# Group 3's x in the first stream of loads, pair 3's selection beside pair 2's, group 2's sums on VectorE, and a new order of VectorE's first steps

## The chip, the core and the metric

The kernel runs on one core of a Trainium2 chip. The core has TensorE (PE in the profile), VectorE (DVE), ScalarE (ACT), GpSimd (POOL) and SyncE (SP), which here issues nearly all transfers; 16 DMA engines carry these out. The metric is device time in microseconds (us). The kernel before has a median of 272.37 us over 3 runs (272.14 to 272.92). A single execution of it was profiled, and all durations below come from that one.

## What is computed

```python
def cond(x, weights, condition):
    W = weights[condition]                       # one 64x64 matrix per batch
    return jnp.einsum('bct,bcd->bdt', x, W)      # x: (64, 64, 1024) float32

def ffn(h, qweight, scale, zero_point, bias):
    w = (unpacked - zero_point) * scale          # unpacked: 6-bit integers, (1024, 1024)
    return jnp.einsum('bsk,nk->bsn', h, w) + bias

out = x + ffn(cond(x, cond_weights, itok), qweight, scale, zero_point, bias)
```

Two products follow each other: a small one with a matrix chosen for each batch, and a large one with quantized weights that are the same for all. The weights stay 6-bit integers in the large product. Their zero point comes in as a correction: the sum of h over its features, times zero point and scale.

## The kernel before, in words

**Tiling.** Two batches of 64 channels make a pair that fills 128 partitions. There are 32 pairs, and two pairs are a group (group g holds pairs 2g and 2g+1). For each pair TensorE does two stages. Stage 1 (line 442; for pairs 0 and 1 line 388) multiplies x by the chosen matrix into PSUM, in a buffer called ph of which there is one from pair 2 on. Stage 2 (line 466) multiplies the result h by the unpacked weights into po, in two banks of 512 columns, with 8 tiles of the contraction. For accuracy h is split into a float16 high part hh (ScalarE, line 454) and a low part hl (VectorE, line 458), and both are multiplied. From pair 2 on x is split in the same way: ScalarE takes magnitudes (line 251), a tiny matmul spreads them (line 255), VectorE makes powers of two (lines 131 to 135), ScalarE writes hf (line 275), VectorE lf (line 285). Four transfers then stack hf and lf into xa (lines 297 to 303), the operand of stage 1.

**The matrices.** The table tab of all 16 matrices is scaled on VectorE (lines 183 and 189). For each pair from 2 on, `select_pair` (line 220) issues two transfers from tab into wst (line 227), one for each batch.

**The sums.** hf's sum over time comes with line 275 as xs. `split_sums` (line 305) splits it into high and low parts xh: ScalarE casts (line 309), then either POOL subtracts (line 311, group 1 alone) or ScalarE does four small activations (line 315). `feature_sums` (line 318, matmuls at line 323) multiplies xh by the chosen matrices, and `unscale_sums` (line 334) scales the result on VectorE.

**The output.** For the first four pairs `early_out` (lines 422 and 426) reads po on VectorE. Later pairs use lines 507 and 512. POOL adds bias and zero points into x (lines 495 and 502), and SP stores.

**The order of work** is written out by hand: each engine executes what the program lists for it, in that order. Lines 533 to 658 are the start, up to the second stage of pair 2 and the first of pair 3. From there `window(p)` (line 663) is called for each pair p from 3 on: TensorE does stage 1 of pair p+1 and then stage 2 of pair p. In windows with even p (p = 2g) the x of group g+3 is loaded and the matrices of group g+2 are selected.

**SP's queue.** SP issues in program order. A transfer takes the semaphore that the eighth transfer before it had, and its issue waits until that one has landed. The first stream (lines 85 to 97) holds, in this order, the condition numbers, the matrices, pair 0's x in two halves, pair 1's x, the weight words in three pieces, the x of pairs 2 and 3, scale and zero point spread over the partitions, and group 2's x. Group 3's x is loaded at line 592, between pair 2's selection and pair 3's pieces of xa; pair 3's selection (line 609) comes behind those pieces.

**The first steps.** 43 dummy matmuls (line 525) keep TensorE busy before x is there. Pairs 0 and 1 use x unsplit with matrices copied by POOL (line 349). VectorE takes the largest weight (line 354), the largest x of the second half (line 368), their product (line 371), and powers from it (line 132); it unpacks the weight words (lines 146 and 148) and writes the low parts of pairs 0 and 1 (line 403).

Of the kernel before, what the change touches and what calls it, by code (L numbers as in the profile page):

```python
# [9 lines left out]
F16 = mybir.dt.float16  # L10
# [4 lines left out]
ALU = mybir.AluOpType  # L15
# [14 lines left out]
def adaln_ffn(ctx: ExitStack, tc: tile.TileContext, x, cond, cw, qw, ws, wz, bias, out):  # L30
# [6 lines left out]
    NG = NP // 2  # L37
    KT = T // P
    LO, HI = slice(0, C), slice(C, P)
    WARM = 43  # L40

    xf = x.rearrange("(i j) c t -> (j c) i t", j=2)
    of = out.rearrange("(i j) c t -> (j c) i t", j=2)
# [23 lines left out]
    def load_x(g):  # L67
        xts[g] = xp.tile([P, 2, T], F32, name="xt")
        nc.sync.dma_start(xts[g], xf[:, 2 * g : 2 * g + 2, :])
# [25 lines left out]
    nc.sync.dma_start(scb, ws.rearrange("n o -> (n o)").partition_broadcast(P))  # L95
    nc.sync.dma_start(zsb, wz.rearrange("n o -> (n o)").partition_broadcast(P))
    load_x(2)


    dummy = const.tile([P, P], BF, name="dummy")  # L100
# [40 lines left out]
    def unpack(kt, n=1):  # L141

        w = kt if kt < 2 else kt - 2 if kt < 6 else kt - 4
        to, of_ = q16[:, kt : kt + n, :], qr[:, w : w + n, :]
        if kt in (2, 3, 6, 7):
            nc.vector.tensor_scalar(to, of_, 6 if kt < 4 else 8, 63, ALU.logical_shift_right, ALU.bitwise_and)  # L146
        else:
            nc.vector.tensor_scalar(to, of_, 63, None, ALU.bitwise_and)  # L148
# [30 lines left out]
    def weights_powers():  # L179
        powers(tmp["pw"], wup, wdn)  # L180
# [39 lines left out]
    def select_pair(p):  # L220
        g, i = divmod(p, 2)
        if i == 0:
            wsts[g] = sp.tile([P, 2, 2, 2, D], F16, name="wst")
        if p not in conditions:
            conditions_of(p)
        for j, k in enumerate(conditions[p]):
            nc.sync.dma_start(wsts[g][:, i, :, j, :], tab[:, ds(k, 1), :, :].rearrange("p o a d -> p (o a) d"))  # L227
# [9 lines left out]
    def magnitudes(g, i):  # L237
        if g not in st:
            st[g] = {
                "l1": sp.tile([P, 2], BF, name="l1"),  # L240
                "u": sp.tile([P, 2], F32, name="u"),
                "hs": sp.tile([P, 2], F32, name="hs"),
                "xs": sp.tile([P, 2], F32, name="xs"),
                "up": sp.tile([P, 2], F32, name="up"),
                "down": sp.tile([P, 2], F32, name="down"),
                "hf": ap.tile([P, 2, T], F16, name="hf"),
                "lf": ap.tile([P, 2, T], F16, name="lf"),
                "xa": ap.tile([P, 2, 2, T], F16, name="xa"),
            }
        junk = ap.tile([P, T], BF, name="junk", bufs=1)  # L250
        nc.scalar.activation(junk, xts[g][:, i, :], AF.Abs, accum_out=st[g]["l1"][:, i : i + 1])  # L251
# [31 lines left out]
    def split_2(g, i, ts_=ALL):  # L283

        nc.vector.scalar_tensor_tensor(  # L285
            st[g]["lf"][:, i, ts_],
            xts[g][:, i, ts_],
            st[g]["down"][:, i : i + 1],
            st[g]["hf"][:, i, ts_],
            ALU.mult,  # L290
            ALU.subtract,
        )
# [9 lines left out]
        nc.sync.dma_start(xa[HI, sl, 0, ts_], lf[LO, sl, ts_])  # L302
        nc.sync.dma_start(xa[LO, sl, 1, ts_], lf[HI, sl, ts_])

    def split_sums(g):
        xs = st[g]["xs"]
        xh = sp.tile([P, 2, 2], F16, name="xh")
        for j, (h, o) in enumerate(((LO, HI), (HI, LO))):
            nc.scalar.copy(xh[h, :, j], xs[h, :])  # L309
            if g == 1:  # L310
                nc.gpsimd.tensor_tensor(xh[o, :, j], xs[h, :], xh[h, :, j], ALU.subtract)  # L311
                continue
            for i in range(2):
                s = slice(i, i + 1)
                nc.scalar.activation(xh[o, s, j], xh[h, s, j], AF.Identity, bias=xs[h, s], scale=-1.0)  # L315
        st[g]["xh"] = xh

    def feature_sums(g):
        xh = st[g]["xh"]
# [31 lines left out]
    def early_weights(p):  # L351

        wl = const.tile([P, 1], F32, name=f"wl{p}")
        nc.vector.tensor_reduce(wl, wbd[:, p, :], AX.X, ALU.max, apply_absolute_value=True)
        nc.vector.tensor_scalar(wm[:, p, :], half, wl[:, 0:1], None, ALU.mult)
# [5 lines left out]
    def early_magnitudes(p, n, ts_, eng):  # L361

        xm[p, n] = const.tile([P, 1], F32, name=f"xm{p}{n}")
        if eng is nc.scalar:
            junk = ap.tile([P, T], BF, name="junk", bufs=1)
            nc.scalar.activation(junk[:, ts_], xts[0][:, p, ts_], AF.Abs, accum_out=xm[p, n])
        else:
            nc.vector.tensor_reduce(xm[p, n], xts[0][:, p, ts_], AX.X, ALU.max, apply_absolute_value=True)

    def early_rows(p, n):  # L370
        nc.vector.tensor_scalar(pb[:, p, n, :], wm[:, p, :], xm[p, n][:, 0:1], LEAST, ALU.mult, ALU.max)
# [14 lines left out]
    def early_stage1(p, ph, kts=range(KT)):  # L386
        for kt in kts:
            nc.tensor.matmul(
                ph[:, kt % ph.shape[1], :, :], lhsT=xts[0][:, p, ts(kt, P)], rhs=wbd[:, p, :], start=True, stop=True
            )  # L390

    def early_high(p, ph, kts):
        if p not in hs_pair:
            hs_pair[p] = [hp.tile([P, KT, P], F16, name="hh"), hp.tile([P, KT, P], F16, name="hl")]
        for j, h in enumerate((LO, HI)):
            nc.scalar.activation(
                hs_pair[p][0][:, kts, h], ph[:, :, j, :], AF.Copy, scale=updown[:, p, 1, j : j + 1]
            )

    def early_low(p, ph, kts):  # L400
        hh, hl = hs_pair[p]
        for j, h in enumerate((LO, HI)):
            nc.vector.scalar_tensor_tensor(  # L403
                hl[:, kts, h], ph[:, :, j, :], updown[:, p, 1, j : j + 1], hh[:, kts, h], ALU.mult, ALU.subtract
            )
# [50 lines left out]
    def stage1_low(p, ph, kts=slice(0, KT)):  # L456
        hh, hl = hs_pair[p]
        nc.vector.tensor_tensor(hl[:, kts, :], ph[:, kts, :], hh[:, kts, :], ALU.subtract)  # L458
# [78 lines left out]
    early_weights(0)  # L537
    early_magnitudes(0, 0, HALF[0], nc.scalar)
    early_stage1(0, ph0a, range(0, 4))
    early_rows(0, 0)  # L540
    early_magnitudes(0, 1, HALF[1], nc.vector)
    early_rows(0, 1)
    early_stage1(0, ph0b, range(4, 6))
    early_bounds(0, 2)
# [1 line left out]
    early_scales(0)  # L546
    early_high(0, ph0a, LOWER)
    early_high(0, ph0b, UPPER)
    unpack(0)
    early_stage1(1, ph1)  # L550
    weights_turn()
    early_weights(1)
    unpack(1)
    early_low(0, ph0a, LOWER)
    stage2_tiles(0, range(0, 2), [0])
    weights_diagonal()
    early_low(0, ph0b, UPPER)
    early_magnitudes(1, 0, ALL, nc.scalar)
    weights_bounds()
    stage2_tiles(0, range(0, 2), [1])  # L560
    early_sums(0)
    unpack(2, 2)
    weights_powers()
    early_rows(1, 0)
    stage2_tiles(0, range(2, 3))
# [22 lines left out]
    unpacking.close()  # L588
    late = ctx.enter_context(tc.tile_pool(name="late", bufs=1))
    select_pair(2)  # L590
    magnitudes(1, 1)
    load_x(3)


    stage2_tiles(1, range(0, 4), [0])
# [10 lines left out]
    stack_low(1, SECOND)  # L606
    early_out(0)
    magnitudes(2, 0)
    select_pair(3)
    nc.sync.dma_start(bib, bias.partition_broadcast(P))  # L610
    select_pair(4)
    select_pair(5)
# [3 lines left out]
    ph = stage1(2)  # L616
    stage1_high(2, ph)
    magnitudes(2, 1)
    split_sums(1)
    stage2_tiles(1, range(7, KT))  # L620
    early_feature_sums(1)
    stage1_low(2, ph)
# [19 lines left out]
    stage1_high(3, ph)  # L642
    early_out(1)
    magnitudes(3, 0)
    magnitudes(3, 1)
    split_sums(2)
    early_zero_points(2)
    stage2_bank(2, 1)
    stage1_low(3, ph)
    split_2(2, 1)  # L650
    stack_high(2, SECOND)
    stack_low(2, SECOND)
# [10 lines left out]
    def window(p):  # L663

        g, i = divmod(p, 2)
        if p + 1 < NP:
            ph = stage1(p + 1)
        if i == 1 and g + 2 < NG:
            bounds(g + 2)
        if i == 1 and g + 1 < NG:  # L670
            feature_sums(g + 1)
        if p - 1 < 4:
            early_out(p - 1)
        else:
            scale_out(p - 1)
        if i == 1 and g + 2 < NG:
            scales_in_full(g + 2)
        if i == 1 and g + 1 < NG:
            unscale_sums(g + 1)
        if p + 1 < NP:  # L680
            stage1_high(p + 1, ph)
        if p - 1 >= 4:
            accumulate(p - 1)
            store(p - 1)
        if p + 1 < NP:
            stage1_low(p + 1, ph)
        if i == 0:
            if g + 3 < NG:
                load_x(g + 3)
            if g + 1 < NG:  # L690
                split_sums(g + 1)
            if g + 2 < NG:
                magnitudes(g + 2, 0)
                magnitudes(g + 2, 1)
            if g + 1 < NG:
                add_bias(p + 2)
                add_bias(p + 3)
            if g + 2 < NG:
                select(g + 2)
        else:  # L700
            if g + 2 < NG:
                for n in range(2):
                    split_1(g + 2, n)
                    split_2(g + 2, n)
                stack_high(g + 2)
                stack_low(g + 2)
            if g + 1 < NG:
                zero_points(p + 1)
                zero_points(p + 2)
        if p in LATE:  # L710

            what, n = LATE[p]
            what(n)
            if what is early_add:
                store(n)
        if p < NP - 1:
            stage2(p)
# [72 lines left out]
```

## Time and profile before

| | |
|---|---|
| median of 3 runs | 272.37 us |
| the profiled execution | 271.98 us |
| its span | 270.2 us |
| TensorE busy | 261.1 us, 97% of the span |
| VectorE, ScalarE, POOL busy | 201.4, 159.3, 166.2 us |
| TensorE busy, by stretches | 5.87 of 6 in 24 to 30, 1.04 of 3 in 30 to 33, 5.26 of 6 in 33 to 39 |
| group 3's x: issue, time to landing | 22.02 us, 7.3 us |
| group 2's x: issue, time to landing | 7.99 us, 11.4 us |
| pair 3's selection: issues, time to landing | 25.29 and 26.04 us, 6.7 and 6.0 us |

The busy row adds up whole stretches with different limits, so a share of 97% doesn't say where the idle 3% lie; the stretches do. A transfer's time to landing is counted from the start of its issue and holds its wait in the queue behind earlier transfers.

### The profile page before, as it was taken

Reading aid. Unit: us, or ns where it says so; the run is one execution under the profiler, and the core shown is the slowest. Engines: PE = TensorE matmul, PEld = TensorE weight load, DVE = VectorE, ACT = ScalarE, POOL = GpSimd, SP = SyncE. Lnnn points to the kernel's source line nnn. Section 1 sums busy time; section 2 is a strip of 40 time slices with the busy share of each in tenths; the row PEclk is TensorE's granted clock in tenths of the full one; section 3 lists DMA queues with packets and bytes.
Section 4 is the critical chain, followed back from the end, with each engine's and each line's share of the span. In section 5 each row is a group of like instructions: output and inputs, shape, how many; then the busy total and the mean of one; then the engine's idle time right before and its main releaser. Section 6 shows DMA issues by size and latency. Waiting matters only on the chain.

```text
span 270.2 us, 5723 instructions
## 1 busy us (share of the span) xinstructions
PE 261.1 (97%) x2161; PEld 140.0 (52%) x2161; DVE 201.4 (75%) x269; ACT 159.3 (59%) x285; POOL 166.2 (61%) x85
## 2 busy tenths in 40 slices
PE   7999789999999999999999999999999999999994
PEld 7645445455555545555554555555455555545553
DVE  3797699498695959869595986959598695955543
ACT  3787698676565667656566765656676565634100
POOL 4000163949689595968959596895919387495200
PEclk9999999999999999999999999999999999999999
DMA  6977876866766797586955797667976764551203
GB/s 220 405 270 183 216 160 190 237 186 186 212 168 231 235 266 238 129 310 187 311 170 158 247 251 238 188 222 243 272 239 173 209 179 146 166 158 78 80 17 139
DMA packets 35708, 54.78 MB, mean 203 GB/s; under 512 B 18400, under 2 KB 18656, under 8 KB 35680
## 3 DMA queue, kind: packets, MB, share of 16 engines
q1 hardware_dynamic: 35648, 54.41, 66.9%
q8 instruction: 17, 0.28, 0.4%
q14 instruction: 11, 0.09, 0.1%
q10 hardware_dynamic: 32, 0.00, 0.0%
HBM read 19.93 MB, written 16.78 MB: 136 GB/s over the span
## 4 chain that ended last, share of the span: by engine, by line
PE 85%; DMA 6%; DVE 4%; SPq 3%; issue 1%
PE po L466 72%; PE ph L442 10%; DMA xt<-in_x_dram 3%; PE pe L466 3%; DMA qr<-in_L_ffn_qweight_dram 2%; DMA xa<-lf 1%; SPq L227 1%; DVE hl L403 1%; PE pu L323 1%; DVE q L148 1%; DVE lf L285 0%; SPq L65 0%; DVE q L146 0%; DVE wsc L183 0%; DVE tab L189 0%
## 5 line engine op out<-in xcount | busy, mean ns | idle before, releaser
L466 PE MATMUL po<-q,hh 128*128 128x512 f16 x496 | 118.5, 379 | 0.4 <-DVE q L146 0.2
L466 PE MATMUL po<-q,hl 128*128 128x512 f16 x496 | 118.5, 379 | 0.0
L502 POOL TENSOR_TENSOR xt<-xt,zt 128x1024 f32<-128x1024 f32 x28 | 78.8, 2833 | 53.1 <-ACT zt L500 53.1
L466 PEld LDWEIGHTS <-hl 128*128 128x128 f16 x520 | 50.6, 98 | 59.1
L495 POOL TENSOR_TENSOR xt<-xt,bib 128x1024 f32<-128x1024 f32 x32 | 75.4, 2379 | 7.5 <-DMA wst<-tab 5.5
L454 ACT CAST hh<-ph 128x1024 f16<-128x1024 f32 x30 | 30.3, 1011 | 82.6 <-PE ph L442 44.8
L466 PEld LDWEIGHTS <-hh 128*128 128x128 f16 x520 | 48.2, 98 | 52.8 <-issue 0.8
L507 DVE SCALAR_TENSOR_TENSOR po<-po,u,scb 128x1024 f32<-128x1024 f32 x27 | 34.7, 1287 | 50.7 <-PE po L466 50.7
L285 DVE SCALAR_TENSOR_TENSOR lf<-xt,down,hf 128x1024 f16<-128x1024 f32 x30 | 62.4, 2117 | 1.8 <-ACT hf L275 1.8
L458 DVE TENSOR_TENSOR hl<-ph,hh 128x1024 f16<-128x1024 f32 x30 | 36.4, 1214 | 0.0
L442 PEld LDWEIGHTS <-xa 128*128 128x128 f16 x960 | 32.1, 98 | 7.9 <-DMA xa<-lf 0.8
L275 ACT ACTIVATE hf<-xt,down 128x1024 f16<-128x1024 f32 x30 | 34.2, 1144 | 2.5 <-DVE down L132 2.5
L512 DVE TENSOR_TENSOR xt<-po,xt 128x1024 f32<-128x1024 f32 x27 | 33.1, 1225 | 2.2 <-DVE po L507 0.5
L442 PE MATMUL ph<-wst,xa 128*128 128x64 f16 x960 | 33.1, 193 | 0.7 <-DMA xa<-lf 0.7
L251 ACT ACTIVATE junk<-xt 128x1024 bf16<-128x1024 f32 x30 | 31.7, 1056 | 1.0 <-DMA xt<-in_x_dram 0.3
L500 ACT ACTIVATE zt<-zsc,hs 128x1024 f32<-128x1024 f32 x28 | 30.5, 1138 | 0.0
L315 ACT ACTIVATE xh<-xh,xs 64x1 f16<-64x1 f16 x56 | 13.4, 287 | 0.9
L311 POOL TENSOR_TENSOR xh<-xs,xh 64x2 f16<-64x2 f32 x2 | 0.4, 194 | 21.0 <-ACT xh L309 20.9
L431 POOL TENSOR_TENSOR xt<-xt,res 128x1024 f32<-128x1024 f32 x4 | 9.4, 2359 | 0.0
L466 PE MATMUL pe<-q,hh 128*128 128x256 f16 (+1 forms) x24 | 6.6, 308 | 0.0
L466 PE MATMUL pe<-q,hl 128*128 128x256 f16 (+1 forms) x24 | 6.5, 308 | 0.0
L334 DVE SCALAR_TENSOR_TENSOR hs<-pu,u 64x2 f32<-64x2 f32 x30 | 4.6, 153 | 1.7 <-PE pu L323 1.6
(83 smaller groups left out, 104.8 us busy)
## 6 DMA issues: line engine op xcount, KB each, us to landing
out_dram<-xt SPq DMA_DIRECT2D x31, 512.0 KB, 3.0
xt<-in_x_dram SPq DMA_DIRECT2D x14, 1024.0 KB, 7.3
xa<-hf SPq DMA_DIRECT2D x26, 256.0 KB, 3.8
xa<-lf SPq DMA_DIRECT2D x26, 256.0 KB, 3.8
wst<-tab SPq DMA_DIRECT2D x60, 32.0 KB, 3.0
xt<-in_x_dram SPq DMA_DIRECT2D x3, 512.0 KB, 7.7
xa<-hf SPq DMA_DIRECT2D x8, 128.0 KB, 2.4
xa<-lf SPq DMA_DIRECT2D x8, 128.0 KB, 3.0
```

The costliest lines, as they stand in the source:

```text
L251: nc.scalar.activation(junk, xts[g][:, i, :], AF.Abs, accum_out=st[g]["l1"][:, i : i + 1])
L275: nc.scalar.activation(st[g]["hf"][:, i, ts_], xts[g][:, i, ts_], AF.Copy, scale=st[g]["down"][:, i : i + 1], accum_out=st[g]["xs"][:, i : ...
L285: nc.vector.scalar_tensor_tensor(st[g]["lf"][:, i, ts_], xts[g][:, i, ts_], st[g]["down"][:, i : i + 1], st[g]["hf"][:, i, ts_], ALU.mult, ...
L442: nc.tensor.matmul(ph[:, kt, j, :], lhsT=st[g]["xa"][:, i, j, ts(kt, P)], rhs=wsts[g][:, i, a, j, :], start=(a == 0), stop=(a == 1),)
L454: nc.scalar.copy(hs_pair[p][0][:, kts, :], ph[:, kts, :])
L458: nc.vector.tensor_tensor(hl[:, kts, :], ph[:, kts, :], hh[:, kts, :], ALU.subtract)
L466: nc.tensor.matmul(po[:, a], lhsT=hs_pair[p][k][:, kt, :], rhs=qT[:, kt, c], start=(kt == 0 and k == 0), stop=(kt == KT - 1 and k == 1),)
L495: nc.gpsimd.tensor_tensor(xt, xt, bib, ALU.add)
L500: nc.scalar.activation(zt, zsc, AF.Copy, scale=st[g]["hs"][:, i : i + 1])
L502: nc.gpsimd.tensor_tensor(xt, xt, zt, ALU.subtract)
L507: nc.vector.scalar_tensor_tensor(po, po, st[g]["u"][:, i : i + 1], scb[:, cols], ALU.mult, ALU.mult)
L512: nc.vector.tensor_tensor(xts[g][:, i, cols], po, xts[g][:, i, cols], ALU.add)
```

## The change

Seven edits. The dummy matmuls grow from 43 to 49. Group 3's x is loaded right behind group 2's, in the first stream. Pair 3's selection is issued right behind pair 2's, ahead of pair 3's pieces of xa. VectorE's first steps are put in another order: the reduction of x's second half ahead of the first row product, pair 1's weights ahead of the first unpacking, and the unpacking of tiles 2 and 3 ahead of the upper half of pair 0's low part. `split_sums` is taken apart into `sums_high` (the two casts) and `sums_low` (the subtraction, on an engine that is given). Group 2's high part stands between the two magnitudes of group 3, and its low part is subtracted on VectorE behind pair 3's hl. Group 1 stays on POOL and groups from 3 on stay on ScalarE, where the two casts now come ahead of the four activations.

```diff
-    WARM = 43
+    WARM = 49
...
     load_x(2)
+    load_x(3)
...
-    def split_sums(g):
-        xs = st[g]["xs"]
-        xh = sp.tile([P, 2, 2], F16, name="xh")
+    def sums_high(g):
+        st[g]["xh"] = sp.tile([P, 2, 2], F16, name="xh")
+        for j, h in enumerate((LO, HI)):
+            nc.scalar.copy(st[g]["xh"][h, :, j], st[g]["xs"][h, :])
+
+    def sums_low(g, eng):
+        xs, xh = st[g]["xs"], st[g]["xh"]
         for j, (h, o) in enumerate(((LO, HI), (HI, LO))):
-            nc.scalar.copy(xh[h, :, j], xs[h, :])
-            if g == 1:
-                nc.gpsimd.tensor_tensor(xh[o, :, j], xs[h, :], xh[h, :, j], ALU.subtract)
+            if eng is not nc.scalar:
+                eng.tensor_tensor(xh[o, :, j], xs[h, :], xh[h, :, j], ALU.subtract)
                 continue
             for i in range(2):
                 s = slice(i, i + 1)
                 nc.scalar.activation(xh[o, s, j], xh[h, s, j], AF.Identity, bias=xs[h, s], scale=-1.0)
-        st[g]["xh"] = xh
...
     early_stage1(0, ph0a, range(0, 4))
+    early_magnitudes(0, 1, HALF[1], nc.vector)
     early_rows(0, 0)
-    early_magnitudes(0, 1, HALF[1], nc.vector)
     early_rows(0, 1)
...
     early_high(0, ph0b, UPPER)
+    early_weights(1)
     unpack(0)
     early_stage1(1, ph1)
     weights_turn()
-    early_weights(1)
     unpack(1)
...
     weights_diagonal()
-    early_low(0, ph0b, UPPER)
     early_magnitudes(1, 0, ALL, nc.scalar)
...
     unpack(2, 2)
+    early_low(0, ph0b, UPPER)
     weights_powers()
...
     select_pair(2)
+    select_pair(3)
     magnitudes(1, 1)
-    load_x(3)
...
     magnitudes(2, 0)
-    select_pair(3)
...
     magnitudes(2, 1)
-    split_sums(1)
+    sums_high(1)
+    sums_low(1, nc.gpsimd)
...
     magnitudes(3, 0)
+    sums_high(2)
     magnitudes(3, 1)
-    split_sums(2)
     early_zero_points(2)
     stage2_bank(2, 1)
     stage1_low(3, ph)
+    sums_low(2, nc.vector)
     split_2(2, 1)
...
             if g + 1 < NG:
-                split_sums(g + 1)
+                sums_high(g + 1)
+                sums_low(g + 1, nc.scalar)
```

## The prediction

> **What bounds the kernel now.** I read three views, in this order. First the chain of waits: from 37.99 us on it is TensorE and nothing else, pair after pair (0.93 us of line 442, 6.9 us of line 466), to the last stores. So whatever this change does in the first 38 us moves the end one for one, unless a later transfer becomes late. Before 37.99 the chain runs through two transfers:
>
> ```profile
> 20.89 0.31 SPq L227
> ...
> 22.02 7.27 DMA xt<-in_x_dram
> 29.28 0.02 issue
> 29.30 0.63 SPq L227
> ...
> 34.19 3.67 DMA xa<-lf
> 37.85 0.14 issue
> 37.99 1.03 PE ph L442 x30
> ```
>
> The reader is to see that group 3's x, not needed by any matmul before 38 us, stands in the chain for 7.27 us: pair 4's selection is the eighth transfer after it, reuses its semaphore and starts at its landing (29.29, then 29.30). Second, TensorE's waits in the first 48 us:
>
> ```profile
> PE pu L323 <- DMA wst<-tab: 2.0, 1, 2.0
> PE pc L525 <- DVE one L103: 1.1, 1, 1.1
> PE ph L388 <- DMA xt<-in_x_dram: 0.8, 1, 0.8
> PE ph L442 <- DMA xa<-lf: 0.7, 2, 0.5
> PE pl L376 <- DVE pb L371: 0.3, 1, 0.3
> PE po L466 <- DVE q L146: 0.2, 1, 0.2
> ```
>
> About 3.2 us of these lie after 7 us (2.0 + 0.7 + 0.3 + 0.2); two that the view doesn't list stand in the timeline, 0.2 us before 14.51 (VectorE's unpacking) and 0.2 us before 26.40 (ScalarE's hh). The rest of TensorE's row is gapless from 7.6 to 30.3 us. Third, the timeline, for who is late at each place:
>
> ```profile
> 6.58 0.67 DVE L368 TENSOR_REDUCE xm<-xt 128x1 f32<-128x512 f32 x1
> 7.57 0.16 PE L376 MATMUL pl<-pb,all_ones 128*128 128x2 bf16 x1 [0.27 <-DVE pb L371]
> ...
> 24.20 1.10 PE L442 MATMUL ph<-wst,xa 128*128 128x64 f16 x32
> ...
> 32.27 0.19 PE L323 MATMUL pu<-xh,wst 128*128 128x2 f16 x2 [1.96 <-DMA wst<-tab]
> ...
> 35.33 1.21 DVE L458 TENSOR_TENSOR hl<-ph,hh 128x1024 f16<-128x1024 f32 x1
> ```
>
> **VectorE's first steps and the warm-up: 0.35 us.** The second half of pair 0's x lands at 6.16 (issued 1.66, 4.5 to landing), but the reduction starts at 6.58, behind the row product of half 0. Put first, it runs 6.17 to 6.85, both products (0.08 us apart when they follow each other, 0.23 long) end near 7.2, and the bounds matmul goes at 7.25 instead of 7.57: 0.32 gained. That the product of half 0 comes later is covered: its matmul stands just ahead of the other. Pair 1's weights (0.28 + 0.23 us) go into the 0.67 us in which VectorE waits for the first quarter of the weight words (landing 8.61), so both unpackings end near 9.5 instead of 9.88; TensorE wants them at 9.9. Unpacking of tiles 2 and 3 goes ahead of the upper half of hl (0.86 us): its words land near 10.7, it ends near 11.5 instead of 12.48, and TensorE's wait of 0.21 goes. What is late next: the upper hl, now ending at 12.3, is needed at tile 4 (14.1); powers and pair 1's row follow at 12.9, and TensorE wants them then; unpacking 4 and 5 ends at 14.1 instead of 14.46, which is where TensorE is held. From there, with no other gap, TensorE reaches line 442 for pair 2 at **23.85** instead of 24.20. Bounds: 0 (the words are late) to 0.5. The six dummy matmuls cost nothing: at the 55 ns spacing of the later ones they take 0.33 us, and TensorE is idle from 4.96 to 5.72, waiting for x. Without that cover: 0.33.
>
> **Group 3's x, moved to the first stream.** Issued at 8.66 instead of 22.02, it follows group 2's x, which lands at 19.4 (7.99 + 11.4). The stream moves 410 GB/s (8 to 16 us), so 1.05 MB are 2.55 us more: it lands near **21.95**. SP's queue then has pair 2's halves of xa (from 17.5) and pair 2's selection (from 20.2) behind it. Here a rule speaks against the change. The row first: in the windows from 17 to 19 us the DMA rate falls to 41 GB/s and below, packet by packet. Most of the engines have finished with group 2's x by 17.4; a late one works to 19. The rule (the Trainium skill, "DMA: Bandwidth & Descriptors", section "Queues, rings and completion order"): on each DMA engine descriptors are consumed in ring order, and only the full count of its semaphore, one from each engine used, says that a transfer has landed. By the mean engine (17.4 + 2.55 = 19.95) x is gone when xa comes, and pair 2 is on time. By rule and latest engine, everything behind x waits for 21.95. The trace of before shows this very queue once: x landed at 29.3, the four pieces of xa from 29.7 to 31.75, the two selections at 32.0 and 32.05, the last 2.75 after x. I take this row: pair 2's selection lands at 24.7, and line 442 for pair 2 starts at **24.75**, 0.55 later than before and 0.9 later than TensorE could. Bounds: 23.85 (mean engine) and 27.4 (if this load costs 5.2 us, as group 4's at 39.04 took from issue to landing, instead of 2.55). The first end is nearer, as the rate of the stream is measured while it is full.
>
> **Pair 3's selection beside pair 2's.** Two issues of 0.73 us each now stand at 21.7 to 23.2, ahead of pair 3's pieces of xa (hf ready at 21.9, issued at 23.2 instead of 22.73); the second waits for the eighth transfer before it, which is now group 3's x (21.95): covered by 0.5. These pieces are wanted at 30.8, and without x before them they land by 28. Pair 3's selection lands near 25.3 instead of 32.05, so the wait of 1.96 at line 323 goes whole. Bias and the selections of pairs 4 and 5 follow without the stop at 29.30 and are issued by 29.5, so pair 4's pieces of xa go when ScalarE and VectorE have them, not after 32.28.
>
> **What is then late next.** With pair 2 at 24.75, ScalarE's hh, the bounds of group 2 and hf, lf of pair 4 all come 0.55 later: lf ends at 31.5. Line 323 runs at 30.65, pair 3's line 442 from 30.85 to 31.8, pair 2's second bank (3.45, from 33.40 to 36.85 before) to 35.25. VectorE after lf: the two scalings at line 334 (0.35), early_out(1) (2.5 from 32.86 to 35.33), hl of pair 3 (1.2): 35.55. Pair 4's line 442 writes the one ph buffer that hl reads, so it can't start before **35.6**. Its last lf is issued at 32.15; 2.3 to landing as at 36.20 gives 34.45, 3.7 as at 34.19 (an instruction load of about 1.4 us sat on one DMA engine from 34 us) gives 35.85. I take 35.6. Before, that stage was torn (2 at 37.29, 30 from 37.99, end 39.02) and its undisturbed 0.95 would start at 38.05.
>
> **Group 2's sums.** On ScalarE two casts (0.37) go between the two magnitudes and four activations of 64x1 (2 x 0.48, about 1.0 us) leave it; on VectorE two operations of 64x2 come behind hl of pair 3, at 0.19 each on POOL in this trace, some 0.3 together. ScalarE has the second magnitude at 36.2, VectorE the sums at 35.9, TensorE asks for both at 36.55: hidden. Left on ScalarE they would end at 37.5 and hold TensorE for about 0.9. The loop's own regrouping (g from 3 on) changes no count.
>
> **Sum.** 35.6 against 38.05: **2.45 us** off. Profiled execution 271.98 (span 270.2 and 1.8 around it): 269.5. The median shown, 272.37, lies 0.4 above that execution, so I forecast **269.9**.
>
> **Rivals.**
> *The mean engine decides* (chance 0.25). Pair 2 starts at 23.85; the chain through lf, early_out(1) and hl ends 0.9 sooner, at 34.65, and stage 442 of pair 4 at 34.7: 3.35 off, 269.0. For it: xa landed in its shortest time, 2.3 us, at 17.84, when the lag had nearly gone. Against it: the 41 GB/s tail.
> *The gain is partly given back at group 3's xa* (0.15). VectorE gains only 1.4 there: hl(3), sums, lf of pair 5, zsc, early_out(2), scales, hl(4) and two lf follow without a gap and end at 44.95 (46.33 before), pieces are issued to 45.65 and land at 4.0, 49.65; TensorE asks at 53.90 - 2.45 = 51.45. An instruction load (as at 46.58, where an issue took 1.97) costs 1.4 and still fits; two delays, or x of group 4 in the way, put it 1.0 late: 270.9.
> *Slower* (0.06). Group 3's x in front of pair 2. If it costs 7.3 us there, as two later 1 MB loads take from issue to landing, it lands at 26.7, pair 2's selection at 29.45 and line 442 starts 4.7 later than forecast: 274.6. It decides from a landing of x at 25.2 on (3.3 later than mine, more than 2.45 + 0.8). Against it: the first stream averages 409 GB/s from 8 to 16 us, and x comes right behind it.
> *The change doesn't do what it says* (0.06): the wait at line 323 belongs to bias or pair 3's xa and stays, 272.4. Against it: the selections landed in queue order behind x.
>
> **How the numbers follow.** Forecast 0.48 (own range 269.4 to 270.4), the rivals as given. The range runs from 268.8 (mean engine with 0.5 from the first steps) to 271.0 (given back). Below 0.3%, about 0.8 us, a measurement of this kernel can't tell a change. Faster 0.88, same 0.06, slower 0.06.
>
> **What would show it.** Landing of group 3's x near 22 and of pair 2's selection near 24.7; a TensorE wait of about 0.9 ahead of pair 2's line 442, none at line 323; pair 4's line 442 at 35.6, whole; TensorE gapless after it. A wait at 51 us for xa, or a landing after 25, makes it wrong.

## The result, and the profile after

The changed kernel has a median of **270.72 us** over 5 runs (270.06 to 270.92), beside 272.37 of the kernel before (5 runs on the same chip, 271.80 to 273.31). The ratio is 0.9931, with a 95% interval of 0.9904 to 0.9958: faster, by 1.65 us at the medians. The forecast was 269.9 with a range of 268.8 to 271.0. The time lies in that range, 0.8 us above the forecast and outside the likeliest case's own range of 269.4 to 270.4. So the direction was right, and the size was put too high: 2.45 us instead of 1.65. One execution of a later kernel (group 2's sums on ScalarE) ran at a granted clock of 0.852 and took 306.26 us; it is left out of that kernel's median.

The profiled execution took 270.72 us, with a span of 268.9 (270.2 before) at a granted clock of 1.000. First TensorE's entries behind 9 us in the view of waits of the changed kernel, which goes from the start to 60 us (engine, line, what it waited for: us in total, times, longest):

```profile
PE ph L445 <- DMA wst<-tab: 1.5, 1, 1.5
...
PE ph L445 <- DVE hl L461: 0.2, 1, 0.2
```

The 2.0 us ahead of the feature sums (line 323 before, 326 now) and the 0.7 us ahead of pair 4 for xa are gone. In their place stands one wait of 1.5 us: pair 2's matrices are late (and its last pieces of xa, at 25.33 us, were hardly sooner). The chain of waits of the changed kernel, from 20.2 to 37.6 us (start, length, what), shows what follows from it:

```profile
20.17 5.32 DMA wst<-tab
...
25.52 1.21 PE ph L445 x32
...
26.76 1.02 ACT hh L457
...
29.76 1.25 ACT hf L276 x2
...
31.04 1.30 DVE lf L286
...
32.71 1.30 DVE po L425
...
34.04 1.22 DVE res L429
35.26 1.14 DVE hl L461
...
36.45 1.14 PE ph L445 x32
```

Read from below: pair 4's stage 1 starts at 36.45, when VectorE has finished pair 3's hl. VectorE works without a gap from lf on, and lf came when the bounds behind pair 2 let it. All of it hangs on pair 2's stage 1 at 25.52, and that on the first of the selection's two transfers, which took 5.32 us from issue to landing. This is the forecast's own chain, with each place some 0.8 us late. SP and TensorE in the timeline of the changed kernel (start, length, engine, line; in brackets the idle time ahead and what ended it), and below it TensorE's entry for pair 4's second stage in the kernel before:

```profile
8.02 1.04 SPq L69 DMA_DIRECT2D xt<-in_x_dram  x2
...
20.17 4.54 SPq L228 DMA_DIRECT2D wst<-tab  x4
...
24.81 0.56 SPq L298 DMA_DIRECT2D xa<-hf  x1
25.52 1.20 PE L445 MATMUL ph<-wst,xa 128*128 128x64 f16 x32 [1.50 <-DMA wst<-tab]
...
36.45 1.14 PE L445 MATMUL ph<-wst,xa 128*128 128x64 f16 x32 [0.25 <-DVE hl L461]
...
37.55 1.89 PE L469 MATMUL po<-q,hh 128*128 128x512 f16 x8
```

```profile
38.99 1.89 PE L466 MATMUL po<-q,hh 128*128 128x512 f16 x8
```

The four issues of the selections of pairs 2 and 3 fill 4.54 us of SP's queue. The fourth reuses the semaphore of group 3's x and stood until that load had landed, at 24.08. Pair 4's second stage starts at 37.55 instead of 38.99. That is 1.44 off. Pair 6's stage 1 at 52.30 takes 1.24 us instead of 1.10, the only later loss. 1.44 - 0.14 is 1.30, which is the difference of the spans (270.2 - 268.9).

**Where the load was late.** A landing is the last of the 16 increments of a transfer's semaphore, which I read as one from each DMA engine. Their times in the trace of the changed kernel and of the kernel before:

| increments, us | median engine | 15th | last |
|---|---|---|---|
| group 2's x, before | 17.88 | 18.26 | 19.39 |
| group 2's x, after | 17.88 | 18.37 | 19.86 |
| group 3's x, after | 20.74 | 21.62 | 24.08 |
| pair 2's selection (first transfer), after | 23.62 | 23.95 | 25.48 |

Fifteen engines had finished group 3's x at 21.62, earlier than the 21.95 of the forecast. One was at 24.08. The trace doesn't name the engine of a packet; I read packets that start where the one before ends as those of one engine. So read, it fell behind at 13.54, where a packet of 16,384 bytes on the instruction queue took 1.108 us (at 14.90 in the trace before, also 1.108). Then, from 20.07 to 23.04 us, nine of its 4,096-byte packets of x took 253 to 454 ns each, where the packets from 18.9 to 19.5 us took 159 to 171. In that stretch the other engines were already copying hf and lf into xa: their packets of 2,048 bytes begin at 19.56, with 84 ns each, and take up to 265 ns later on.

### The profile page after: what moved, and what is told of

It reads as the page before. It is cut to its first block, busy times and chain, and to the rows that moved or that the text cites. A ratio compares the mean times of both kernels' runs of the same rounds, so it can differ in the third digit from the quotient of the medians.

```text
span 268.9 us, 5732 instructions
## 1 busy us (share of the span) xinstructions
PE 261.4 (97%) x2167; PEld 140.3 (52%) x2167; DVE 201.9 (75%) x271; ACT 158.0 (59%) x281; POOL 166.1 (62%) x85
## 4 chain that ended last, share of the span: by engine, by line
PE 88%; DVE 5%; DMA 4%; ACT 1%; SPq 0%; issue 0%
PE po L469 74%; PE ph L445 10%; PE pe L469 3%; DMA xt<-in_x_dram 2%; DMA wst<-tab 2%; DVE lf L286 1%; PE ph L391 1%; PE pu L326 1%; DVE hl L406 0%; DVE po L425 0%; ACT hf L276 0%; DVE res L429 0%; DVE hl L461 0%; DVE wsc L184 0%; ACT hh L457 0%
## 5 line engine op out<-in xcount | busy, mean ns | idle before, releaser
L461 DVE TENSOR_TENSOR hl<-ph,hh 128x1024 f16<-128x1024 f32 x30 | 36.4, 1215 | 0.0
L445 PE MATMUL ph<-wst,xa 128*128 128x64 f16 x960 | 33.2, 193 | 1.8 <-DMA wst<-tab 1.5
L252 ACT ACTIVATE junk<-xt 128x1024 bf16<-128x1024 f32 x30 | 31.7, 1056 | 1.4 <-DMA xt<-in_x_dram 0.7
L319 ACT ACTIVATE xh<-xh,xs 64x1 f16<-64x1 f16 x52 | 12.4, 287 | 0.5
L309 ACT CAST xh<-xs 64x2 f16<-64x2 f32 x30 | 5.7, 192 | 0.4
```

The source lines that it names most:

```text
L445: nc.tensor.matmul(ph[:, kt, j, :], lhsT=st[g]["xa"][:, i, j, ts(kt, P)], rhs=wsts[g][:, i, a, j, :], start=(a == 0), stop=(a == 1),)
```

## The experiments

All times are medians, and each ratio is against runs of the kernel before on the same chip (medians 272.44 to 272.64). Unless said otherwise an edit starts from the changed kernel.

**Group 3's x behind group 2's stacking.** The load leaves the first stream and comes in the middle of the old order; all else of the change stays.

```diff
     load_x(2)
-    load_x(3)
...
     stack_low(1, SECOND)
+    load_x(3)
     early_out(0)
```

> The changed kernel with one edit: group 3's x is loaded behind pair 3's pieces of xa instead of in the first stream. Theory (x in front of pair 2's pieces and selection makes them late, by the one late DMA engine): pair 2's selection lands near 22.5 to 23.2 us, line 445 for pair 2 starts at 23.9 instead of 25.5, line 445 for pair 4 near 34.8 instead of 36.45, and the time falls by about 1.6 us against the changed kernel, to about 269.1. Rival (what is missing of the forecast lies in VectorE's chain of early_out and hl, not in x): pair 2 starts earlier but pair 4's line 445 stays near 36.4 and the time stays at 270.7.

Measured: 271.93 us (14 runs, 270.13 to 273.64), ratio 0.9978 [0.9952, 1.0003]: most of the gain is lost at the median. The timeline of this kernel:

```profile
24.54 1.10 PE L444 MATMUL ph<-wst,xa 128*128 128x64 f16 x32
...
36.77 0.23 PE L444 MATMUL ph<-wst,xa 128*128 128x64 f16 x2 [1.66 <-DMA xa<-lf]
37.26 1.08 PE L444 MATMUL ph<-wst,xa 128*128 128x64 f16 x30 [0.26 <-DMA xa<-lf]
```

Pair 2's selection has landed at 23.61 (25.64 in the profile after) and TensorE doesn't wait for it, so it was the load that had held it. TensorE itself comes later in this execution, at 24.54 (the second half of pair 0's x landed at 7.30 here and at 6.13 in the profile after). But now x lands at 31.7, the bias behind it at 33.2, and pair 4's pieces of xa between 36.4 and 37.1: the load pushes whatever is behind it, and here that is pair 4.

**Group 3's x behind both selections**, ahead of pair 3's pieces:

```diff
     load_x(2)
-    load_x(3)
...
     select_pair(3)
     magnitudes(1, 1)
+    load_x(3)
```

> The changed kernel with group 3's x back ahead of pair 3's pieces of xa, but behind both selections. Theory (the move of x is needed, the selection's place alone is worth little): pair 2's line 445 at 23.9, the pieces of pair 3 land behind x near 32, stage 1 of pair 3 starts there, the stop of SP for x's landing comes back; time 271.5 to 272.4. Rival (the gain is the selection's new place, 1.96 us of the wait at line 323): 270.4 or less.

Measured: 273.04 us (14 runs), ratio 1.0018 [1.0000, 1.0037]. This is nearly the kernel before with pair 3's selection moved alone (the first steps and the sums are the new ones), so the selection's new place gives nothing by itself. The wait at the feature sums goes, and one as long comes at the next stage:

```profile
30.68 0.24 PE L325 MATMUL pu<-xh,wst 128*128 128x2 f16 x4
33.20 0.29 PE L444 MATMUL ph<-wst,xa 128*128 128x64 f16 x2 [2.28 <-DMA xa<-lf]
...
35.64 3.60 PE L468 MATMUL po<-q,hh 128*128 128x512 f16 x8
```

The last line holds a second finding. Eight matmuls of 128x512 take 3.60 us here and 1.89 elsewhere. The windows view of this kernel has the granted clock in the number ahead of the last two (span, busy time of each engine, PEclk, DMA share, GB/s):

```profile
30.00:40.00 10.00, 7.17 (x51) 3.77 (x50) 7.11 (x10) 6.46 (x13) 2.37 (x2) 0.66 0.83 186
```

The mean clock in this window, in which the wait lies, is 0.66. Of the 14 executions of each of these two kernels, 7 and 9 had a mean clock of 0.994 or less over the whole span, and these are the slower ones without exception (in the first: 272.24 to 273.64 against 270.13 to 271.62). The kernel before shows it as well: in 25 of its 71 executions beside the experiments the mean clock is 0.994 or less, and their median is 273.08 us against 272.24 of the other 46. The changed kernel's five are all at 1.0. So the first experiment needs a second look: its seven executions at the higher clock have a median of 270.98, near the changed kernel, and most of what it loses at the median is lost with the clock. For the second, the five at the higher clock have 272.21, against 272.37 of the kernel before on the same chip: still no gain.

**The same with the wait filled.** 48 dummy matmuls keep TensorE busy where the kernel just described waits:

```diff
+    pf = ps_s.tile([P, P], F32, name="pf", tag="s")
+    for _ in range(48):
+        nc.tensor.matmul(pf, lhsT=dummy, rhs=dummy, start=True, stop=True)
     ph = stage1(3)
```

> The run with group 3's x put back (273.04, clock at 0.985 to 0.994 in 9 of 14 executions) with 48 dummy matmuls, 2.7 us, in TensorE's wait ahead of pair 3's stage 1. Theory (a TensorE wait of about 2 us costs its clock for the next 1.5 to 3 us, in the executions that show a clock below 0.995): the clock is 0.997 or more in nearly all executions and the time falls to 271.4 to 272.4, with pair 3's stage 1 near 33.5 as before. Rival (the lower clock comes from elsewhere): clock below 0.995 in half of the executions, time 273 or, by the added work, more.

Measured: 272.06 us (22 runs), ratio 0.9984 [0.9970, 0.9998]: 1.0 us less than without the dummies, though work was added, and close to the 272.21 of that kernel's executions at the higher clock. The clock was 0.996 or more in all 22 executions. The timeline of this kernel at the same place:

```profile
33.30 0.22 PE L444 MATMUL ph<-wst,xa 128*128 128x64 f16 x2
33.75 1.05 PE L444 MATMUL ph<-wst,xa 128*128 128x64 f16 x30 [0.23 <-DMA xa<-lf]
34.64 1.89 PE L468 MATMUL po<-q,hh 128*128 128x512 f16 x8
```

The pieces of xa are as late as before, yet the next eight matmuls take 1.89 us.

**The load's move alone**, on the kernel before:

```diff
     load_x(2)
+    load_x(3)
...
     magnitudes(1, 1)
-    load_x(3)
```

> The kernel before with one edit: group 3's x in the first stream. Theory (x's place makes the whole gain; the selection's place, the sums and the first steps are hidden): pair 2's line at 24.5 to 25.5, no wait at the feature sums of group 1, pair 4's stage 1 near 36.2, time 270.3 to 270.9 as the changed kernel. Rival (pair 3's selection must stand beside pair 2's for the gain): the wait at line 323 stays above 1 us, 271.6 or more.

Measured: 270.34 us (6 runs), ratio 0.9924 [0.9902, 0.9947]: the whole gain of the change, within the intervals. Its timeline:

```profile
24.72 1.10 PE L443 MATMUL ph<-wst,xa 128*128 128x64 f16 x32
...
30.65 0.24 PE L324 MATMUL pu<-xh,wst 128*128 128x2 f16 x4
...
35.62 1.19 PE L443 MATMUL ph<-wst,xa 128*128 128x64 f16 x32 [0.32 <-DVE hl L459]
```

There is no wait at the feature sums, although pair 3's selection is still behind pair 3's pieces: without x in front it lands at 28.0, in time for 30.65. Pair 2 and pair 4 start within 0.03 us of the 24.75 and 35.6 of the forecast. In this execution x landed at 22.94, and TensorE itself was later (the second half of pair 0's x landed at 7.25, and at 6.13 in the profile after).

**VectorE's old first steps**, with 43 dummy matmuls and the order of before:

```diff
-    WARM = 49
+    WARM = 43
...
-    early_magnitudes(0, 1, HALF[1], nc.vector)
     early_rows(0, 0)
+    early_magnitudes(0, 1, HALF[1], nc.vector)
...
-    early_weights(1)
     unpack(0)
...
+    early_weights(1)
     unpack(1)
...
+    early_low(0, ph0b, UPPER)
     early_magnitudes(1, 0, ALL, nc.scalar)
...
-    early_low(0, ph0b, UPPER)
```

> The changed kernel with VectorE's old order of first steps and 43 dummy matmuls. Theory (pair 2 waits for transfers until 25.5 us, which covers what the first steps gain): tile 4 of pair 0 is reached 0.33 later, but line 445 for pair 2 still starts near 25.5; time 270.7, within 0.2. Rival (the 0.35 us of the first steps is on the path to the end): 271.05 and line 445 for pair 2 near 25.85.

Measured: 270.75 us (6 runs), ratio 0.9937 [0.9917, 0.9957], against 270.72 with the new order. Hidden, as the expectation had it: pair 2's matrices decide here too, though barely.

```profile
25.04 1.22 PE L445 MATMUL ph<-wst,xa 128*128 128x64 f16 x32 [0.17 <-DMA wst<-tab]
```

**Group 2's sums left on ScalarE**, behind the second magnitude of group 3:

```diff
-    sums_high(2)
     magnitudes(3, 1)
+    sums_high(2)
+    sums_low(2, nc.scalar)
...
-    sums_low(2, nc.vector)
```

> The changed kernel with group 2's sums split on ScalarE behind the second magnitude of group 3, as before the change. As forecast, TensorE would be held at the feature sums for 0.9 us: 271.6. By the changed kernel's trace, ScalarE would end them near 37.5 and TensorE asks at 37.45: 0.1 us, time 270.8.

Measured: 270.24 us (5 runs), ratio 0.9927 [0.9904, 0.9949]. No cost can be seen, where the prediction had 0.9 us. The timeline of ScalarE and TensorE:

```profile
24.55 1.10 PE L445 MATMUL ph<-wst,xa 128*128 128x64 f16 x32
...
35.44 1.14 PE L445 MATMUL ph<-wst,xa 128*128 128x64 f16 x32 [0.32 <-DVE hl L461]
35.64 0.99 ACT L319 ACTIVATE xh<-xh,xs 64x1 f16<-64x1 f16 x4
36.50 0.37 PE L326 MATMUL pu<-xh,wst 128*128 128x2 f16 x4
```

ScalarE ends these sums at 36.6, and TensorE asks at 36.5: the four small matmuls are stretched from 0.24 to 0.37 us, and that is all.

**Do the copies into xa slow x?** Seven transfers of 64 bytes behind x shift the semaphores, so that the first piece of xa takes the one of x and can't start before x has landed:

```diff
     load_x(3)
+    scrap = const.tile([1, 7, 16], F32, name="scrap")
+    for n in range(7):
+        nc.sync.dma_start(scrap[:, n, :], ws.rearrange("n o -> o n")[:, 0:16])
```

> The changed kernel with seven transfers of 64 bytes between group 3's x and pair 2's pieces of xa, so that the first piece takes x's semaphore and is issued only when x has landed. Theory (x's last packets run at half speed or less because the other engines copy the pieces within SBUF at that time): without the copies x lands 2.5 to 3.2 us after group 2's x, near 22.5, and no 4 KB packet after 19.9 takes over 200 ns. Rival (a late engine is slow by itself, or the memory is): x lands at 23.5 to 24.1, 3.8 us or more after group 2's. Pair 2 starts near 27.5 in either case, and the time is 272 or more.

Measured: x landed at 21.66, 2.48 us behind group 2's x (19.18), and no 4,096-byte packet behind 19.0 us took over 168 ns. With the copies beside it the same megabyte took 4.22 us on its last engine, and packets there up to 454 ns. The first piece was issued at 24.44. So neither a late engine by itself nor the memory makes the second part of the delay; it is what runs beside x. This run holds back the selections as well as the copies, but in the profile after the packets of x are slow from 20.0 on, when the copies' packets are under way and the selections' packets of 128 bytes (from 21.55) are not. That leaves the copies as the cause, by one execution of this kernel. As a whole it is slower (277.21 us), since its pieces now wait:

```profile
29.12 0.27 PE L448 MATMUL ph<-wst,xa 128*128 128x64 f16 x2 [4.09 <-DMA wst<-tab]
```

**Half of x early.** If the load's size on its last engine is what is left to win, half of it should win most of that:

```diff
     load_x(2)
-    load_x(3)
+    load_pair(6)
...
     stack_low(1, SECOND)
+    load_pair(7)
```

> The changed kernel with group 3's x in two halves: pair 6's 0.5 MB in the first stream, pair 7's behind pair 3's pieces of xa. Theory (each byte ahead of pair 2's selection makes it late, each byte behind pair 3's pieces makes pair 4's pieces late, since the DMA engines are full from 24 to 36 us): the half lands near 21.5 and pair 2's selection near 23.3, so line 445 for pair 2 goes when TensorE gets there (23.9 to 24.5); pair 4's line 445 lies between 35.0 and 35.9; no clock below 0.995; time 269.3 to 270.2. Rival (pair 4's pieces are late whichever part of x is behind): a wait over 1.5 us at pair 4's line 445 with the clock halved after it, 271.5 or more.

Measured: **270.21 us** (6 runs, 269.72 to 270.29), ratio 0.9907 [0.9887, 0.9928], the lowest median of all. Its interval overlaps that of the changed kernel, so a gain over it is not shown. The half landed at 20.52, and the timeline shows pair 2 on time and a new loss later:

```profile
24.43 1.10 PE L445 MATMUL ph<-wst,xa 128*128 128x64 f16 x32
...
35.32 1.18 PE L445 MATMUL ph<-wst,xa 128*128 128x64 f16 x32 [0.31 <-DVE hl L461]
...
52.07 1.05 PE L445 MATMUL ph<-wst,xa 128*128 128x64 f16 x30 [0.64 <-DMA xa<-lf]
```

The 0.64 us at 52 us is the place of the rival "given back at group 3's xa".

**The bias later as well**, behind pair 4's pieces of xa, to free the queue in front of them (an edit of the halves):

```diff
-    nc.sync.dma_start(bib, bias.partition_broadcast(P))
     select_pair(4)
...
     stack_low(2, FIRST)
+    nc.sync.dma_start(bib, bias.partition_broadcast(P))
```

> As the run with halves, and the 0.5 MB of spread bias are loaded behind pair 4's pieces of xa instead of ahead of pair 4's selection. Theory: 1.3 us of transfers leave the way of pair 4's pieces, which land by 34.5; line 445 for pair 4 waits for hl of pair 3 alone, at 34.8 to 35.3; 269.0 to 269.6. Rival (VectorE is as late, or POOL's late bias comes back at the end): 270 or more.

Measured: 270.54 us (6 runs), ratio 0.9930 [0.9906, 0.9955]. Not faster than the halves alone, and the theory's 269.0 to 269.6 is missed. Pair 4 starts at 35.19, released by VectorE's hl (0.32 us of wait) as with the halves, so the queue was not what held it.

**VectorE's order behind pair 2.** As VectorE's chain sets pair 4, pair 3's hl was put between the two scalings of `early_out(1)`, and the product zsc went to POOL, early:

```diff
+    nc.gpsimd.tensor_tensor(zsc, zsb, scb, ALU.mult)
...
-    early_out(1)
+    early_out_1(1)
...
     stage1_low(3, ph)
...
+    early_out_2(1)
...
-    nc.vector.tensor_tensor(zsc, zsb, scb, ALU.mult)
```

It was tried on the halves, on the halves with the old first steps, and on the changed kernel with the whole x:

> The kernel with group 3's x in halves, and VectorE relieved where it came out late: hl of pair 3 stands between the two scalings of early_out(1) (so ph is free 1.2 us sooner, and po is still free before pair 3's second stage), and the product of zero points and scales, 1.2 us, is made on POOL, idle then. Theory (VectorE's chain sets pair 4's stage 1 and then group 3's xa): pair 4's line 445 at 34.9 instead of 35.3, no wait above 0.2 at pair 6's line 445 near 51; 0.9 us less than with halves alone: 269.3 or less. Rival (transfers set it, VectorE is only close): pair 4's pieces hold it at 35.3 or later and the wait at 51 stays 0.4 or more; 270.0 to 270.3.

> As the run before, with VectorE's old order of first steps and 43 dummies. With pair 2's selection in time, the first steps should be on the path: 0.35 us slower than that run, pair 2's line 445 0.3 to 0.4 later. Rival (still hidden, or swamped by when x lands): within 0.15.

> The changed kernel (group 3's x whole in the first stream) with VectorE relieved in the same way. Theory: 0.5 to 0.9 us less than the changed kernel, 269.8 to 270.2, and 0.3 to 0.9 more than with halves, by pair 2's wait for its selection. Rival (pair 2's selection is all that counts): 270.7.

Measured: 270.87 (7 runs), 270.70 (6) and 271.04 us (12); ratios 0.9937 [0.9916, 0.9958], 0.9935 [0.9913, 0.9957] and 0.9948 [0.9932, 0.9964]. All three theories are missed: the first and the third are not faster than the kernels that they start from (270.21 and 270.72), and the second, with the old first steps, is not slower than the first. On the halves VectorE and POOL show a loss in front of pair 2 (POOL's first row and VectorE's two):

```profile
18.16 2.36 POOL L543 TENSOR_TENSOR zsc<-zsb,scb 128x1024 f32<-128x1024 f32 x1 [11.56 <-DMA zsb<-n_weight_zero_point_dram]
18.32 3.29 DVE L286 SCALAR_TENSOR_TENSOR lf<-xt,down,hf 128x1024 f16<-128x1024 f32 x1
21.53 1.21 DVE L190 TENSOR_TENSOR tab<-wsc,tab 128x1024 f16<-128x1024 f32 x1
```

VectorE's lf takes 3.29 us beside POOL's product, and 1.28 at this place in the profile after. The table tab, from which the matrices are selected, is then ready at 22.74 instead of 19.9. This profile is of the slowest of the seven executions (272.35 us), so it doesn't measure the loss of a usual one. In the profiles of the other two kernels lf took 1.65 and 2.33 us. With the whole x the new order did its work at pair 4, which starts at 35.49 without a wait for hl, 10.59 us behind pair 2 (10.93 in the profile after), and the gain was given back at pair 6:

```profile
35.49 1.27 PE L451 MATMUL ph<-wst,xa 128*128 128x64 f16 x32
...
52.86 1.03 PE L451 MATMUL ph<-wst,xa 128*128 128x64 f16 x30 [0.98 <-DMA xa<-lf]
```

The order without POOL's product was not tried, so what each of the two moves is worth stays open.

## Why the forecast was right in direction and too large

**The chain: right.** Pair 2's selection holds pair 2's stage 1, VectorE's row follows from it, pair 3's hl releases pair 4's stage 1, and both old waits are gone. The trace after and the load's move alone show it with the same releasers.

**The step that was sized wrong: the load's price behind group 2's x.** The forecast took 2.55 us more and a landing at 21.95. On the last engine it was 24.08, which is 2.13 late: 0.47 because group 2's x was itself later there (19.86 against 19.39), and 1.67 because that engine's share of x took 4.22 instead of 2.55. A part came back: the selection's two transfers followed x by 1.40 and 1.56 instead of 2.75, and fifteen engines had the first of them at 23.95, before x had landed on the last. So pair 2 started 0.77 later than forecast (25.52 against 24.75) and pair 4 0.85 later (36.45 against 35.6). From there to stage 2 it took 1.10 instead of the 0.94 in the forecast's sum; the feature sums' four matmuls, about 0.10, stand in between. That is 1.44 gained instead of 2.45.

**The rule that was weighed: right, and the row was sized too low.** The Trainium skill ("DMA: Bandwidth & Descriptors", "Why a DMA increments its semaphore by 16 and not by 1") has a transfer landed at the full count of the semaphore and not before. The trace agrees: the median engine was through with x at 20.74, the last at 24.08, and the issue that reuses the semaphore stood until then. The rival "mean engine" had 19.95, too early even for the median, and took that for the landing. The forecast followed the latest engine but let it run at the stream's rate.

**The size differs between executions.** Profiles of four kernels in which x landed at 22.81, 22.94, 23.36 and 24.08 (sums on ScalarE, load alone, old first steps, the change) have pair 2 at 24.55, 24.72, 25.04 and 25.52, and spans of 268.0, 268.1, 269.1 and 268.9. The profile after is the latest of these landings, and it differs from the first three in one more way: the second half of pair 0's x landed at 6.13 there and at 7.32, 7.25 and 7.23 in them. TensorE reached pair 2 early and waited 1.50 us in the profile after, and came later by itself in the first two, with no wait. How much of the 0.8 us that the median lies above the forecast is the load's price, and how much such a later start, is not shown. The forecast's starts of pair 2 and pair 4 are met in the load's move alone, but by luck: x landed 0.99 later than forecast there (22.94), and the selection followed it by 1.68 (24.62) instead of 2.75.

**What the forecast had no term for: the clock.** The kernel before loses some 0.8 us in about a third of its executions, those with a mean clock of 0.994 or less, and the changed kernel has none of these among its five. So a part of the gain at the medians can come from the clock; the profile before, at a clock of 1.000, doesn't show it.

**First steps: right, and worth nothing that could be measured.** TensorE reached pair 2's stage 1 at 23.9 to 24.0 (forecast 23.85), and the two bounds matmuls ran from 7.07 to 7.33 (forecast 7.25 for the second). The old order costs 0.03 us at the medians.

**Pair 3's selection: half right.** The wait at the feature sums did go, but not through the selection's new place: the load's move alone removes it, and the selection's move without it gives nothing (1.0018). Nor was the second issue's wait for x "covered by 0.5": pair 3's pieces were issued at 24.81, not 23.2. It cost nothing, since pair 3's stage 1 started at 31.66 without a wait.

**Group 2's sums: wrong.** Hidden on VectorE, as said, but 0.9 us on ScalarE was not there; about 0.1 was. ScalarE ended the sums at 36.6, where the forecast had 37.5.

**Given back near 51 us: the right place, a smaller price.** 0.14 us in the profile after, 0.65 with the old first steps, 0.64 with the halves, against 1.0 in the rival; with VectorE's new order and the whole x it was 0.98. The slower rival's point of decision, a landing of x behind 25.2, was missed by 1.1 us.

## What to carry to other kernels

A load that nothing needs soon still has a price: it can delay whatever is behind it on its slowest DMA engine, as here. So ask of each place in the queue what stands next there, and size the load by the last engine and not by the stream's rate, above all where copies between buffers will run beside its tail. Try the parts of a change one by one: here one moved line held the whole gain of seven edits, as far as the runs can tell. When a wait only moves from one stage to the next, as with pair 3's selection, removing it at the first place gains nothing.

## What the runs showed of the hardware beyond that

- **A wait of about 2 us on TensorE can cost more than itself.** Behind a wait of 2.28 us eight matmuls took 3.60 us instead of 1.89, with a clock of 0.50 in each microsecond from 33 to 39. Behind a wait of 1.66 us (first experiment) they took 3.46; there the clock was still 1.00 from 37 to 38 us, with TensorE at work again, and fell to 0.56 from 38 to 39. It struck in 7 and 9 of 14 executions. With dummy matmuls in the wait it struck in none of 22.
- **One instruction packet can set back a DMA engine's whole stream.** 16,384 bytes took 1.108 us, and the landings of the stream behind it, up to group 2's x, were 1.1 to 1.5 us later on the last engine than on the 15th (in the profiles before and after).
- **Packets from memory slow down beside copies within the chip**: 253 to 454 ns for 4,096 bytes on the late engine beside the copies into xa, at most 168 without them.
- **VectorE's lf hardly moved beside POOL's product.** In three kernels lf began inside POOL's product (float32, 128x1024), which ended at 20.52, 18.97 and 19.15 us; lf ended at 21.61, 20.05 and 20.24, each time 1.08 to 1.09 later, although it takes 1.28 alone. When lf came first, it took its 1.28 and POOL paid: on the halves with VectorE's new order, lf ran from 59.69 to 60.97, and POOL's addition that began at 59.75 took 3.43 us instead of 2.36. The changed kernel's loop has both in it: the lf at 58.05 began inside POOL's addition and took 3.42.
